# Windowed attention: key sums moved between the key blocks, scores on four 64x64 tiles, division after the values

## The chip, the core and the metric

The kernel runs on one core of a Trainium2 chip. A core has four compute engines that run side by side, each through its own queue in order: TensorE (PE: matmuls; its weight loads are listed apart as PEld), VectorE (DVE), ScalarE (ACT) and GpSimd (POOL). SyncE (SP) starts transfers. Operands lie in on-chip memory of 128 partitions; TensorE writes its results to PSUM, from where VectorE or ScalarE fetch them. The metric is the device time of one execution in microseconds, lower is better. Everything is 32-bit floating point.

## The reference

Two layers run over `x` of shape (2, 1024, 256). The change is in the attention of the second layer, and this is its reference, cut:

```python
# L = 1024, bl = 128, nb = 8 blocks, G = 64 groups of 16 tokens, H = 16 heads, dh = 64
q = einsum('bld,dhk->blhk', x, Wq) / sqrt(dh)
k = einsum('bld,dhk->blhk', x, Wk);  v = einsum('bld,dhk->blhk', x, Wv)
g = einsum('bld,lg->bgd', x, one_hot)          # sums of 16 tokens
side_k = einsum('bgd,dhk->bghk', g, Wk);  side_v = einsum('bgd,dhk->bghk', g, Wv)
# a block of queries sees its own key block, the one before, the one after, and all 64 side keys
k_cat = concatenate([k of 3 blocks, side_k]);  v_cat = ...
logits = einsum('bnqhd,bnkhd->bnhqk', qb, k_cat) + where(|distance| <= 127 and inside, 0, -1e9)
m = maximum(logits.max(-1), 0)
probs = exp(logits - m) / (exp(logits - m).sum(-1) + exp(-m))
y = einsum('bnhqk,bnkhd->bnqhd', probs, v_cat)
out = einsum('blhk,hkd->bld', y, Wo)
```

A query sees keys up to 127 places away on either side. So of the two neighbour blocks, a query at place i of its block sees the last 127 - i keys of the one before and the first i keys of the one after.

## The kernel before

The stage is `attn1` (line 1427) with `attn1_heads` (line 1538). `attn1` goes over the two batches. For each it first projects keys: for each m (a pair of heads, 8 in all) two products of 512 columns into `pq` (line 1498), copied by ScalarE to `kT` (line 1499), and the key sums `pg` from the token sums `g` (line 1504), copied to `sk`. In `kT` the 64 rows of a pair's first head are partitions 0 to 63, those of the second 64 to 127. Then it projects values (`pv`, line 1512) into `v` with keys on partitions, and the value sums into `sv` (line 1526), which holds zeros in the half that does not belong to a head. In the second batch, steps of the next adapter run beside the key projection.

`attn1_heads` then goes over 32 items: 8 query blocks n, and in each the pairs of heads m = 0, 2, 4, 6, two pairs (four heads) to an item. An item passes three steps, and the steps of three items are staggered: in one turn come `scores` of item i, `turn` of item i - 1 and `values` of item i - 2.

- `scores`: for each pair a PSUM tile `ps` of two banks, one per head. Two matmuls (line 1597), each 64 rows deep and 128 queries wide, multiply the queries with 384 keys (an inner block) or 256 (n = 0 and n = 7, called edge items here); two more (line 1601) with the 64 key sums. In an inner block, VectorE then merges one neighbour block into the place of the other where the latter is masked (predicated copies, lines 1603 and 1604), so that 320 columns are left of 448. A reduction (line 1607) adds the mask, negates and finds the maximum; ScalarE takes the exponential with its sum (line 1617), and of the maximum (`extra`). VectorE adds and inverts (`rd`, lines 1623 and 1624), and the weights `pe` are multiplied by it, the first head's on VectorE (line 1625), the second's on ScalarE (line 1626).
- `turn`: TensorE transposes the weights, ten times 128x128 an item (lines 1639 and 1640), into `pt` and `pts`. ScalarE copies the first block and the sums (lines 1643, 1649); VectorE takes the merged neighbours apart again by two products with triangles `tri` (line 1646).
- `values`: for each pair and block, the two heads' matmuls, side by side on 64 columns of the array each (line 1666), accumulate into `py`, the key sums' part last. `py` is one PSUM buffer, taken anew every second item, and ScalarE copies it to `yT` then (line 1678).

After every fourth item in turn, TensorE has a block of projections: the queries of the next two n (`queries`, lines 1564 to 1571, called before the scores of m = 4 of an odd n), or the output of the last two (`output`, lines 1688 to 1691, called behind the values of m = 6 of an odd n). Both use the two buffers of `ps`.

No order is written out by hand beyond the stagger. The framework in which the kernel is written puts in the waits and plans each engine's order: program order, with instructions that it expects to be ready earlier pulled ahead. A tile's next writer waits until its readers are done.

Of the kernel before, what the change touches and what calls it, by code (L numbers as in the profile page):

```python
# [1419 lines left out]

def load_attn1(k, pool, names):
    for n in names:
        k.w1a[n] = pool.tile([P, 2048], F32, name=f"w1a{n}")
        k.nc.sync.dma_start(out=k.w1a[n], in_=part(k.ins["w1a"], W1A, n))


def attn1(k, ci, x):
# [7 lines left out]
    with tiles(tc, name="a1r", bufs=1) as rp:  # L1435

        tri = rp.tile([P, 2, P], F32, name="tri")
        nc.gpsimd.memset(tri, 1.0)

        wbs = rp.tile([P, 4, G + 2 * P + G], F32, name="wbs")
        nc.gpsimd.memset(wbs, 0.0)
        for i in range(2):
            sign = 1 - 2 * i
            nc.gpsimd.affine_select(
                out=tri[:, i],
                in_=tri[:, i],
                compare_op=ALU.is_gt,
                fill=0.0,  # L1450
                base=0,
                pattern=[[-sign, P]],
                channel_multiplier=sign,
            )
        left, right = slice(G, G + P), slice(G + P, G + 2 * P)
        for t, op, sign in (
            (wbs[:, 0, right], ALU.is_gt, -1),
            (wbs[:, 1, right], ALU.not_equal, 1),
            (wbs[:, 2, left], ALU.not_equal, 1),
            (wbs[:, 3, left], ALU.is_gt, 1),  # L1460
        ):
            nc.gpsimd.affine_select(
                out=t, in_=t, compare_op=op, fill=-1.0e9, base=0, pattern=[[sign, P]], channel_multiplier=-sign
            )

        near = rp.tile([P, 2, P], U8, name="near")
        for i, t in enumerate((wbs[:, 3, left], wbs[:, 0, right])):
            nc.vector.tensor_scalar(near[:, i], t, 0.0, None, ALU.is_ge)
        for b in range(B):
            kT = rp.tile([P, 8, S], F32, name="kT")  # L1470
            v = rp.tile([P, NB, 1024], F32, name="v")

            g = rp.tile([P, 2, 2, G], F32, name="g")
            sk = rp.tile([P, 8, G], F32, name="sk")

            sv = rp.tile([P, 8, 2, 64], F32, name="sv")
            nc.gpsimd.memset(sv, 0.0)
            for c in range(2):
                nc.vector.reduce_sum(
                    g[:, c, 0, :], ci[:, c, b * S : (b + 1) * S].rearrange("p (g t) -> p g t", t=16), axis=AX.X  # L1480
                )
            nc.vector.tensor_copy(g[:, :, 1, :], g[:, :, 0, :])
            with ExitStack() as st:
                pp = st.enter_context(tiles(tc, name="a1a", bufs=2 if b else 3, space=PSUM))
# [6 lines left out]
                for m in range(8):  # L1491
                    ms = slice(m * P, (m + 1) * P)
                    for half in range(2):
                        ts = slice(b * S + half * CK, b * S + (half + 1) * CK)
                        ls = slice(half * CK, (half + 1) * CK)
                        pq = pp.tile([P, CK], F32, name="pq")
                        for c in range(2):
                            nc.tensor.matmul(pq, lhsT=wk[:, c, ms], rhs=ci[:, c, ts], start=c == 0, stop=c == 1)  # L1498
                        nc.scalar.copy(kT[:, m, ls], pq)
                    if beside:  # L1500
                        next(beside[m // 4])
                    pg = pp.tile([P, G], F32, name="pg", bufs=1 if b else 2)
                    for c in range(2):
                        nc.tensor.matmul(pg, lhsT=wk[:, c, ms], rhs=g[:, c, 0, :], start=c == 0, stop=c == 1)
                    nc.vector.tensor_copy(sk[:, m, :], pg)
                for half in range(2):
# [17 lines left out]
                    for i in range(2):  # L1524
                        rows = slice(i * G, (i + 1) * G)
                        nc.vector.tensor_copy(
                            sv[rows, 4 * half : 4 * half + 4, i],
                            pv[rows].rearrange("p (m i d) -> p m i d", i=2, d=64)[:, :, i],
                        )
            with (  # L1530
# [4 lines left out]
                attn1_heads(k, b, x, ci, kT, v, sk, sv, (wbs, near, tri), rp, sp, pp, yp)  # L1535
# [432 lines left out]
```

## Time and profile before

| | us |
|---|---|
| median of 3 runs | 1516.82 |
| lowest, highest | 1510.14, 1517.79 |
| the profiled execution | 1515.27 |
| its span, first to last instruction | 1513.6 |
| key projection of batch 0 begins | 876 |
| scores of batch 0, first and last item begin | 945, 1140 |
| scores of batch 1, first and last item begin | 1237, 1434 |

The two sweeps of `attn1_heads` are thus about 400 us of the span. The granted clock is 1.00 in all stretches from 875 us on. Times in the order of time count from the start of the span; the second number in such a line is a duration, "64x384" is partitions by elements, "64*128" the rows and columns of the array that a matmul uses. A 32-bit matmul leaves two records, a transpose one, and records overlap, since TensorE starts the next before the last has left: what one costs is read from start to start. In the chain that ended last, each piece is the time until the next piece could go on.

### The profile page before, as it was taken

To read this page: it belongs to the slowest core of one execution; us is meant where nothing else is said; L and a number is where in the kernel's file an instruction comes from. 1 tells how busy PE (TensorE), PEld (TensorE's weight loads), DVE (VectorE), ACT (ScalarE), POOL (GpSimd) and SP (SyncE) were. 2 spreads that over 40 slices of the span, in tenths; PEclk is the share of its full clock that TensorE was granted. 3 is DMA by queue.
4 is the path that set the end of the run, shared out by engine and by line. 5 is a ranking of instruction groups with operands and counts; after the bars stand their busy time and mean duration, and the time that the engine had idled before them with its cause. 6 is when DMAs were issued, how large, how long until landed. Compare 5 with 4: busy or idle time off the path is not lost. (4 is left out here: it accounts for less than half of the span.)

```text
span 1513.6 us, 27333 instructions
## 1 busy us (share of the span) xinstructions
PE 1414.6 (93%) x10778; PEld 964.2 (64%) x10778; DVE 872.7 (58%) x2774; ACT 680.9 (45%) x1681; POOL 180.7 (12%) x167
## 2 busy tenths in 40 slices
PE   5998889999699999968999999999999999999998
PEld 2445877445456766635666645788886457878866
DVE  3545834121489931157887713787884247778764
ACT  2443143222122122117888721766674337656733
POOL 1523630022411121110000000000000000000011
PEclk9899589999899999979999999999999999999999
DMA  9500004300353332030000010000000000000001
GB/s 307 188 1 2 5 2 154 125 30 30 95 166 120 127 129 82 18 121 1 2 2 2 29 56 1 2 2 2 1 2 1 0 0 2 2 1 2 2 15 44
DMA packets 42758, 70.77 MB, mean 47 GB/s; under 512 B 7168, under 2 KB 35840, under 8 KB 39552
## 3 DMA queue, kind: packets, MB, share of 16 engines
q1 hardware_dynamic: 35776, 55.55, 11.0%
q0 software_dynamic: 3072, 8.65, 1.6%
q10 hardware_dynamic: 3776, 4.75, 1.0%
q8 instruction: 87, 1.43, 0.4%
q14 instruction: 47, 0.39, 0.1%
HBM read 45.09 MB, written 23.86 MB: 46 GB/s over the span
## 5 line engine op out<-in xcount | busy, mean ns | idle before, releaser
L1617 ACT ACTIVATE pe<-pe,nm 128x320 f32<-128x320 f32 x256 | 141.8, 555 | 131.1 <-DVE nm L1607 130.9
L1607 DVE CUSTOM_DVE_ANT_0 pe<-ps,wbs 128x320 f32<-128x320 f32 x256 | 118.5, 486 | 6.1 <-PE ps L1601 1.8
L1229 ACT ACTIVATE pe<-pe,nm 128x256 f32<-128x256 f32 x256 | 110.4, 498 | 20.4 <-DVE nm L1219 20.4
L965 PE MATMUL ph<-xt,w 128*128 128x512 f32 x256 | 113.8, 602 | 2.7 <-ACT xt L960 2.7
L1597 PE MATMUL ps<-kT,qT 64*128 64x384 f32 (+1 forms) x512 | 110.2, 498 | 3.3 <-DVE qT L1571 2.9
L973 PE MATMUL po<-w,h 128*128 128x256 f32 x512 | 111.8, 379 | 0.0
L973 PEld LDWEIGHTS po<-w,h 128*128 128x128 f32 x512 | 97.3, 190 | 16.6 <-issue 3.3
L1219 DVE CUSTOM_DVE_ANT_0 pe<-ps,lc 128x256 f32<-128x256 f32 x256 | 94.2, 417 | 21.0 <-PE ps L1203 19.3
L1666 PE MATMUL py<-ptt,v 128*64 128x128 f32 x1408 | 103.6, 277 | 0.1
L895 DVE SCALAR_TENSOR_TENSOR lc<-iok,idx,lc 128x256 f32<-128x256 f32 x248 | 102.2, 475 | 0.3
L965 PEld LDWEIGHTS ph<-xt,w 128*128 128x128 f32 x256 | 48.6, 193 | 62.6 <-issue 55.7
L1666 PEld LDWEIGHTS py<-ptt,v 128*64 128x64 f32 x1408 | 78.6, 137 | 11.3 <-issue 8.3
L1639 PE MATMUL pt<-ident,pe 128*128 128x128 f32 x512 | 79.8, 282 | 1.9 <-DVE pe L1625 0.9
L1238 PE MATMUL ptp<-ident,pe 128*128 128x128 f32 x512 | 73.8, 283 | 5.7 <-ACT pe L1229 2.9
L1238 PEld LDWEIGHTS ptp<-ident,pe 128*128 128x128 f32 x512 | 55.8, 142 | 33.1 <-ACT pe L1229 16.8
L968 ACT ACTIVATE h<-ph,vecs 128x512 f32<-128x512 f32 x64 | 44.0, 687 | 71.3 <-PE ph L965 70.2
L1626 ACT ACTIVATE pe<-pe,rd 128x320 f32<-128x320 f32 x128 | 70.8, 558 | 8.9 <-DVE rd L1624 8.9
L1601 PEld LDWEIGHTS ps<-sk,qT 64*128 64x128 f32 x512 | 50.9, 187 | 26.2 <-issue 0.3
L1646 DVE TENSOR_TENSOR ptt<-pt,tri 128x512 f32<-128x512 f32 x96 | 64.8, 675 | 0.0
L1639 PEld LDWEIGHTS pt<-ident,pe 128*128 128x128 f32 x512 | 56.1, 140 | 10.9 <-issue 2.0
L976 DVE TENSOR_TENSOR ye<-po,b 128x256 f32<-128x256 f32 x32 | 13.4, 419 | 82.4 <-PE po L973 82.4
L1688 PE MATMUL ps<-yT,w1ao 128*128 128x256 f32 x256 | 59.0, 385 | 0.7
(355 smaller groups left out, 2743.5 us busy)
## 6 DMA issues: line engine op xcount, KB each, us to landing
w<-in_mw SPq DMA_DIRECT2D x16, 1024.0 KB, 5.2
xs<-z SPq DMA_DIRECT2D x8, 1088.0 KB, 11.8
ys<-z SPq DMA_DIRECT2D x4, 1024.0 KB, 11.6
xe<-xs SPq DMA_DIRECT2D x7, 544.0 KB, 6.3
more<-xs SPq DMA_DIRECT2D x7, 544.0 KB, 4.0
x<-in_xT ACTq DMA_DIRECT2D x4, 512.0 KB, 5.9
g<-ys ACTq DMA_DIRECT2D x4, 512.0 KB, 6.0
out_x<-o SPq DMA_DIRECT2D x8, 256.0 KB, 2.2
```

Of the source, the lines that this page charges most:

```text
L895: nc.vector.scalar_tensor_tensor(n, key, k.idx[:, qb, j : j + 1], n, ALU.is_equal, ALU.add)
L965: nc.tensor.matmul(ph, lhsT=w1[:, c, m * P : (m + 1) * P], rhs=xt[:, c, :], start=c == 0, stop=c == 1)
L973: nc.tensor.matmul(po, lhsT=h[:, m, j * P : (j + 1) * P], rhs=w2[:, m, :], start=m == 0, stop=m == 7)
L1219: nc.vector.tensor_tensor_reduce(out=pe[:, j, :], in0=it["ps"][i][:, j, :], in1=k.lc[:, q0 + j, :], scale=-1.0, scalar=3.0e38, op0=ALU.add ...
L1229: nc.scalar.activation(pe[:, j, :], pe[:, j, :], AF.Exp, bias=nm, scale=-1.0)
L1238: nc.tensor.transpose(ptp[:, kb, j, :], it["pe"][i][:, j, kb * P : (kb + 1) * P], k.ident)
L1597: nc.tensor.matmul(ps[:, i, keys[i]], lhsT=qs[i], rhs=kT[hp, m + pair, k0 : k0 + nk], start=True, stop=True)
L1607: nc.vector.tensor_tensor_reduce(out=pe[:, i], in0=ps[:, i, used[i]], in1=wbs[:, 0 if n == 0 else 3 if n == NB - 1 else 1 + i, (1 - i) * G ...
L1617: nc.scalar.activation(pe[:, i], pe[:, i], AF.Exp, bias=nm[:, i : i + 1], scale=-1.0, accum_out=den[:, i : i + 1])
L1626: nc.scalar.activation(pe[:, 1], pe[:, 1], AF.Copy, scale=rd[:, 1:2])
L1639: nc.tensor.transpose(pt[1 - j if i and inner(n) else j][:, 2 * pair + i, :], pe[:, at : at + P], k.ident)
L1666: nc.tensor.matmul(py[64 * i : 64 * i + 64, (m + pair) % 4, :], lhsT=keys[:, hs], rhs=it["pts"][:, pair, :] if j == 3 else it["pt"][:, j, ...
```

## The change

1. `kT` grows by 256 columns, and each head gets its own order of columns, with copies of the 64 key sums between key blocks, so that for every query block a run of 448 columns (320 at the edges) holds its key blocks and one copy of the sums. A class `Keys` holds the two orders; `view` finds, for a head and a block, where the run starts, which 320 columns are used, and which block is merged into which.
2. The key sums come no longer from a matmul with `g`, but from a reduction of `pq` over 16 tokens on VectorE; ScalarE copies the first head's rows of `pq`, VectorE the second's, and GpSimd copies the sums into `kT` after m = 3 and m = 7. `g` and `sk` live only while projecting.
3. Scores: four matmuls a pair, one for each head and half of the queries, each on a 64x64 quarter of the array. A half of the queries leaves out the 64 keys at the far end that are masked for all of it, so that most have 384 columns with the sums in them (320 at the edges).
4. The merge becomes two predicated copies per head, one of all 128 queries by 64 keys, one of 64 by 64.
5. The weights are not divided. Addition and reciprocal are done once an item for four heads; ScalarE spreads the reciprocals over 64 columns a head (`rdw`); two more transposes in `turn` turn them into the second half of `pts`.
6. The key sums' values become a step `sums` of their own, before `turn`: four matmuls on 64x64 quarters, which open the accumulation; `sv` loses its zeros. `py` is one tile for the whole batch. After its last block, each item's two slots of `py` are multiplied by the turned reciprocals into `yT`, by VectorE.
7. The query scaling moves from VectorE to ScalarE; `tri` goes, and the triangle masks `near` (one byte each) take its place.

```diff
+class Keys:
+    def __init__(self, order):
+        self.at, self.sums, at = {}, [], 0
+        for n in order:
+            if n is None:
+                self.sums.append(at)
+                at += S // 16
+            else:
+                self.at[n] = at
+                at += P
...
+KEYS = [Keys([0, 1, None, 2, 3, None, 4, 5, None, 6, 7]), Keys([None, 0, 1, 2, None, 3, 4, None, 5, 6, 7, None])]
...
+def window(n):
+    first = 0 if n == 0 or n in (1, 3, 5) else 1
+    return [KEYS[i].view(i, n, first ^ i) for i in range(2)]
...
-            kT = rp.tile([P, 8, S], F32, name="kT")
+            kT = rp.tile([P, 8, S + 4 * G], F32, name="kT")
...
-                        pq = pp.tile([P, CK], F32, name="pq")
+                        pq = pp.tile([P, CK], F32, name="pq", bufs=3)
...
-                        nc.scalar.copy(kT[:, m, ls], pq)
+                        nc.vector.reduce_sum(sk[:, m, gs], pq.rearrange("p (g t) -> p g t", t=16), axis=AX.X)
+                        for i in range(2):
+                            hp = slice(64 * i, 64 * i + 64)
+                            for n0, n1 in KEYS[i].runs(4 * half, 4 * half + 4):
...
+                                copy = nc.vector.tensor_copy if i else nc.scalar.copy
+                                copy(kT[hp, m, at : at + w], pq[hp, o : o + w])
...
-                    pg = pp.tile([P, G], F32, name="pg", bufs=1 if b else 2)
-                    for c in range(2):
-                        nc.tensor.matmul(pg, lhsT=wk[:, c, ms], rhs=g[:, c, 0, :], start=c == 0, stop=c == 1)
-                    nc.vector.tensor_copy(sk[:, m, :], pg)
+                    if m % 4 == 3:
+                        for i in range(2):
+                            hp = slice(64 * i, 64 * i + 64)
+                            for at in KEYS[i].sums:
+                                nc.gpsimd.tensor_copy(kT[hp, m - 3 : m + 1, at : at + G], sk[hp, m - 3 : m + 1])
...
-            nc.vector.tensor_scalar_mul(qT[:, m : m + 4, :], pq, 0.125)
+            nc.scalar.activation(qT, pq, AF.Copy, scale=0.125)
...
+            for half in range(2):
+                qs = slice((n % 2) * P + half * 64, (n % 2) * P + half * 64 + 64)
+                for hp, view in zip(hps, views):
+                    c0, c1 = view.parts[half]
+                    nc.tensor.matmul(
+                        ps[hps[half], view.head, c0:c1],
+                        lhsT=rows["qT", n // 2, m // 4][hp, (m + pair) % 4, qs],
+                        rhs=kT[hp, m + pair, view.start + c0 : view.start + c1],
...
+                    both, one = (slice(0, 64), slice(64, P)) if view.kind == 0 else (slice(64, P), slice(0, 64))
+                    for rs, cs in ((slice(0, P), both), (one, one)):
+                        nc.vector.copy_predicated(
+                            ps[rs, i, to + cs.start : to + cs.stop],
+                            near[rs, view.kind, cs],
+                            ps[rs, i, of + cs.start : of + cs.stop],
+                        )
...
-            nc.vector.tensor_scalar_mul(pe[:, 0], pe[:, 0], rd[:, 0:1])
-            nc.scalar.activation(pe[:, 1], pe[:, 1], AF.Copy, scale=rd[:, 1:2])
+        nc.vector.tensor_add(rd, den, extra)
+        nc.vector.reciprocal(rd, rd)
+        it["rd"] = sp.tile([P, 4, 64], F32, name="rdw")
+        nc.scalar.copy(it["rd"], rd.unsqueeze(2).to_broadcast([P, 4, 64]))
...
+        for pair in range(2):
+            rd = it["rd"][:, 2 * pair : 2 * pair + 2].rearrange("p i d -> p (i d)")
+            nc.tensor.transpose(pts[:, 1, pair, :], rd, k.ident)
...
-                nc.vector.tensor_mul(ptt[:, 1 + i], pt[1], tri[:, i : i + 1, :].to_broadcast([P, 4, P]))
+                nc.vector.tensor_mul(ptt[:, 1 + i], pt[1], near[:, i : i + 1, :].to_broadcast([P, 4, P]))
...
+    py = yp.tile([P, 4, P], F32, name="py")
+    def sums(it):
...
+                nc.tensor.matmul(
+                    py[64 * view.head : 64 * view.head + 64, (m + pair) % 4, :],
+                    lhsT=sv[hs, views[0].place, m + pair, :],
+                    rhs=it["pts"][hs, 0, pair, :],
+                    start=pair == 0,
...
-            nc.scalar.copy(rows["yT"][:, m - 3 : m + 1, ns], py)
+        nc.vector.tensor_mul(rows["yT"][:, m : m + 2, ns], py[:, m % 4 : m % 4 + 2], it["pts"][:, 1])
...
-    staggered(items, scores, turn, values)
+    for i in range(len(items) + 2):
+        for j, step in ((0, scores), (2, sums), (1, turn), (2, values)):
+            if 0 <= i - j < len(items):
+                step(items[i - j])
```

## The prediction

> **What bounds the kernel now.** I read the busy shares first, then the granted clock, then the stage by its stretches, then the order of time on each engine, then the chain that ended last.
>
> ```profile
> PE 1414.6 (93%) x10778; PEld 964.2 (64%) x10778; DVE 872.7 (58%) x2774; ACT 680.9 (45%) x1681; POOL 180.7 (12%) x167
> ```
>
> TensorE is busy 93% of the span, VectorE 58%. That average says little about this stage. From 945 us on, the table by stretches (us, PE, PEld, DVE, ACT, POOL busy, clock) has this line for a stretch of items without a query or output block:
>
> ```profile
> 1010.00:1026.00 16.00, 16.00 (x197) 13.23 (x192) 15.38 (x61) 13.09 (x44) 0.00 (x0) 1.00 0.01 2
> ```
>
> TensorE is busy for 16.00 of 16.00 us, but VectorE for 15.38 as well, at full clock. The order of time shows both, for one inner item (two pairs of heads), TensorE first:
>
> ```profile
> 1016.17 0.92 PE L1597 MATMUL ps<-kT,qT 64*128 64x384 f32 x4
> 1016.92 0.33 PE L1601 MATMUL ps<-sk,qT 64*128 64x64 f32 x4
> 1017.09 0.87 PE L1597 MATMUL ps<-kT,qT 64*128 64x384 f32 x4
> 1017.79 0.34 PE L1601 MATMUL ps<-sk,qT 64*128 64x64 f32 x4
> 1018.05 0.66 PE L1639 MATMUL pt<-ident,pe 128*128 128x128 f32 x4
> ...
> 1019.29 0.88 PE L1666 MATMUL py<-ptt,v 128*64 128x128 f32 x12
> 1020.00 0.39 PE L1666 MATMUL py<-ptts,sv 128*64 128x128 f32 x4
> 1020.22 0.83 PE L1666 MATMUL py<-ptt,v 128*64 128x128 f32 x12
> ...
> 1021.19 0.92 PE L1597 MATMUL ps<-kT,qT 64*128 64x384 f32 x4
> ```
>
> From start to start: scores 1.88 us (16.17 to 18.05), transposes 1.24, values 1.90, together 5.02 per item. VectorE in the same time:
>
> ```profile
> 1012.59 0.29 DVE L1603 COPY_PREDICATED ps<-near,ps 128x128 f32<-128x128 uint8 x1
> 1012.91 0.30 DVE L1604 COPY_PREDICATED ps<-near,ps 128x128 f32<-128x128 uint8 x1
> 1013.24 0.49 DVE L1607 CUSTOM_DVE_ANT_0 pe<-ps,wbs 128x320 f32<-128x320 f32 x1
> ...
> 1017.91 0.29 DVE L1603 COPY_PREDICATED ps<-near,ps 128x128 f32<-128x128 uint8 x1
> ```
>
> Its item takes 5.32 us, 0.3 more than TensorE's. It falls behind by 0.3 per item, and catches up only in the blocks of 7.2 us of projection that TensorE runs after every fourth item, the queries (L1564) and the outputs (L1688) in turn. The chain that ended last shows that this is already just enough in one burst of two: between a query block and an output block it runs on VectorE, then over ScalarE's copy of the result into the output:
>
> ```profile
> 1034.56 0.30 DVE ps L1603
> ...
> 1051.29 0.49 DVE pe L1607
> ...
> 1055.49 0.49 ACT yT L1678
> ...
> 1056.03 5.45 PE ps L1688 x24
> ```
>
> So TensorE bounds the bursts that end in queries, and VectorE those that end in an output.
>
> **TensorE, part by part.** (1) Scores. The two records of 384 columns of a pair take 0.75 and 0.70 us, the key sums 0.17 to 0.26 behind them. Now four 64x64 tiles of 384 columns do both. That four such tiles run at once is seen in the first attention: there 39 records of 64x32 (L432, such tiles in the same order) took 1.29 us, although one lasts 0.29. I take 0.70 and 0.65 for the pairs. (2) The key sums' values leave the second block (L1666 on ptts, 0.22 per pair) and become four 64x64 matmuls of the same 128 columns behind the scores: 0.44, plus 0.1 for the change to transposes. Scores with sums are then 1.89 against 1.88, and values lose 0.44. (3) Two transposes more, at 0.11 each (four took 0.44 from 1018.65 to 1019.09): +0.22. An inner item goes from 5.02 to about 4.80. In the 16 edge items the scores keep 320 columns where they had 256 and 64, and the same terms cancel: 0. (4) The projection of key sums (L1504) goes: eight key records fill 3.44 us and the next m begins 3.88 after the last, so 0.44 x 16 = 7.0 us.
>
> **VectorE, per inner item.** Each merge becomes two of 64 columns, 8 instead of 4. They don't overlap what follows (0.33 from start to start for a duration of 0.29). A 64-column merge isn't in the trace: its price lies between the reciprocal on 2 columns (0.16) and the 128-column merge (0.29); I take 0.225, by the 64-column copy from PSUM (L1505, 0.220), so 0.26 from start to start: 8 x 0.26 - 4 x 0.33 = +0.76. The weights' scaling goes (0.30 from start to start, twice): -0.60. One addition and reciprocal for four heads, not two: -0.15. The product into yT (128x256 from PSUM, like L552, 0.418, less the overlap of some 0.05) is new: +0.37. Together 5.32 + 0.38 = 5.70; with the ends for the merge 5.2 to 6.2. The query scaling (1.22, L1571) leaves VectorE, but it ran inside the query block, where VectorE idles: nothing gained.
>
> **ScalarE and GpSimd.** ScalarE loses two scalings (0.56 each) and the yT copy (0.58 per two items), and gains the reciprocal broadcast (256 columns, 0.36), 256 more columns in the ptts copy (0.21), and the query scaling, which holds the second score buffer after a block as VectorE's did (0.52 before): lighter, no bound. GpSimd gets 14 small copies of key sums per batch, two groups of seven; at the 0.3 to 1.1 us of its rows they end under the 30 us of value projection. It loses a memset and tri. No DMA changes.
>
> **Key projection.** Per m TensorE has 3.44 us. VectorE gets two reductions of 512 columns (0.69 each, by L1518) and four 64-partition copies (0.56 and 0.29): 3.1 us, where it was busy 1.34 of 20. In batch 1 the adapter adds about 1 us per m on either engine. Three buffers cover it: 0, and 2 us of loss if not.
>
> **Where the stalls go.** An inner item of 4.80 against 5.70 makes VectorE fall behind by 0.9 per item rather than 0.3. Three things are in its favour: the weights reach the transposes without the scaling behind them, the query scaling is gone, and the reciprocals are needed last. Against it stands a new wait: py is now one tile for the whole batch, and yT is made from it for every item by VectorE. The next item's key sums write py, so they wait for that product; behind them on TensorE stand the transposes and the values. Before, ScalarE read py every second item, and TensorE waited for it 0.6 us in all. From the last value matmul to the next sums lie only the next scores, 1.35 us, less 0.3 until VectorE sees the result and 0.4 of product.
>
> I take that wait to hold for the whole of py, although the next item writes other slots of it.
>
> The Trainium skill has a rule here (PSUM — Partial Sum Buffer, "PSUM bank collisions raise a hardware error"): engines are to be kept apart by bank, not by address. The four slots of py fill one 2 KiB bank, so by the page even another slot's product holds the sums back; were it by slot, the bursts ending in queries below would gain 0.9 each instead of losing 0.6, and the sum would be 6 us lower.
>
> Burst from queries to output (six times): first merge 0.98 after the first scores, then four VectorE items of 5.70 to the product that the output needs, or three and the fourth's four merged reductions (4 x 0.93) and the product, if that is ordered first: 0.98 + 21.2 to 22.8 = 22.2 to 23.8. Now the output starts 20.6 after those scores (1033.31 to 1053.9). That is +1.6 to +3.2; I take the middle, 2.4, because the planner does change the order where VectorE is late (at 1251 us it put transposes between the matmuls of two score pairs): +14.4. Bursts from output to queries (four times): nothing needs the last product, but the sums of items two to four need the one before. VectorE ends the products at 6.7, 12.4 and 18.1 after the first scores; TensorE wants them at 6.15, and then, each 4.80 after the last wait, at 11.6 and 17.3: waits (with 0.1 of signalling) of 0.65, 0.9 and 0.9, so 4 x 4.80 + 2.45 = 21.6 where it is 20.0 now: +1.6. If the transposes, which don't need py, are put ahead of the sums, most of it goes: +0.2. I take 0.6: +2.4. Other inner items (8): -1.8. Shorter start of the two batches: -1. Key sums' projection: -7.0. **Sum: +7.0 us**, on the profiled execution's 1515.27 us (span 1513.6 and 1.7 around it), which is 1.55 under the median of the runs, 1516.82: **1522 us**, with a range of its own from 1513 to 1532.
>
> **Rivals.** *TensorE stays the bound* (0.26): merges at the low end, or an order in which VectorE's lag is always hidden: 48 x 0.22 + 7.0 + 1.5 = 19 less, 1496 us. For it: over eight items VectorE needs 46 us of TensorE's 53. It decides once a VectorE item is under about 5.3. This is the side of a gain. *VectorE sets every inner item* (0.20): the product stands behind the next item's merges, so that bursts ending in queries pay too: 48 x (5.70 - 5.02) = 33, less 9: 1539. The stretch with DVE 15.38 of 16.00 speaks for it, the idle 7 us blocks against. *The tiles don't run four at once* (0.04): a pair pays its 0.65 twice, 48 x 2 x 0.65 + 16 x 2 x 0.5 = 78 more: about 1600; L432 speaks against it.
>
> A rule weighed: TensorEngine Tiling (Array Packing), "PSUM Bottleneck", says that tiling speeds up TensorE but not the emptying of PSUM. The trace agrees in this stage (5.32 against 5.02). Taken as the whole truth it gives the second rival's 1539; the trace's blocks give 1522.
>
> **How the numbers follow.** My case 0.50, the rivals 0.26, 0.20, 0.04. Half a per cent, about what a measurement of this kernel can tell from no change, is 7.6 us. Of my case, 0.03 lies below 1509, 0.28 within, 0.19 above 1524. Faster 0.29, same 0.28, slower 0.43. The range takes in the first two rivals: 1494 to 1539.
>
> **What would show it.** Right: pairs of scores 0.7 us apart with eight records; VectorE items of 5.6 to 5.8; TensorE idle before the sums or the output, released by VectorE's yT; no L1504. Wrong: a 64-column merge under 0.19 us, TensorE without gaps at 4.8 (first rival), or score pairs of 1.3 us (third).

## The result: 0.6% slower, near the forecast, with another wait behind it

| | us |
|---|---|
| before, median (lowest, highest) | 1515.61 (1510.14, 1524.36) |
| after, median (lowest, highest) | 1524.97 (1523.03, 1527.70) |
| ratio, with its 95% interval | 1.0056 (1.0038 to 1.0074) |
| profiled execution of after, and its span | 1523.03, 1521.3 |

The forecast was 1522, so the sum came out 3 us off. Two of its steps were wrong, and they are the ones worth reading about: TensorE does wait for VectorE, but at another place than forecast, and VectorE's item is long for another reason.

To see where the time went, the stage is cut at the first records of its steps: start of a key projection, first scores, first scores of an inner block (n = 1), of the last edge block (n = 7), and of the last item. In us:

| | before | after | difference |
|---|---|---|---|
| projection before the first scores, batch 0 | 68.94 | 66.35 | -2.59 |
| first four items (n = 0) | 16.59 | 15.11 | -1.48 |
| the 24 inner items | 164.95 | 172.28 | +7.33 |
| first to last item of n = 7 | 13.40 | 14.21 | +0.81 |
| last item to the next projection | 17.31 | 17.73 | +0.42 |
| projection, batch 1 | 79.14 | 77.55 | -1.59 |
| first four items | 15.25 | 16.22 | +0.97 |
| the 24 inner items | 169.07 | 172.18 | +3.11 |
| first to last item of n = 7 | 13.40 | 14.21 | +0.81 |
| last item to the last output | 15.79 | 16.20 | +0.41 |

Together +8.2: the two sweeps over the items +11.6, the projections -4.2, the ends +0.8. The spans differ by 7.7; the rest lies outside these stages: the stage begins 2.4 us earlier in the trace of after, and what follows the last output takes 2.0 longer, with the same code in both.

### The profile page after: what moved, and what is told of

It is laid out like the page before. It is cut to its first block, busy times and chain, and to the rows that moved or that the text cites. A ratio compares the mean times of both kernels' runs of the same rounds, so it can differ in the third digit from the quotient of the medians.

```text
span 1521.3 us, 27492 instructions
## 1 busy us (share of the span) xinstructions
PE 1404.2 (92%) x10842; PEld 919.8 (60%) x10842; DVE 893.6 (59%) x2846; ACT 664.6 (44%) x1569; POOL 189.0 (12%) x189
## 5 line engine op out<-in xcount | busy, mean ns | idle before, releaser
L1641 PE MATMUL ps<-kT,qT 64*64 64x384 f32 (+2 forms) x1024 | 109.7, 494 | 21.2 <-DVE nm L1662 18.2
L1654 DVE COPY_PREDICATED ps<-near,ps 64x64 f32<-64x64 uint8 (+1 forms) x384 | 79.5, 226 | 39.4 <-PE ps L1641 32.0
L1735 PE MATMUL py<-ptt,v 128*64 128x128 f32 x1408 | 91.0, 277 | 0.0
L1735 PEld LDWEIGHTS py<-ptt,v 128*64 128x64 f32 x1408 | 75.5, 137 | 10.7 <-issue 10.7
L1641 PEld LDWEIGHTS ps<-kT,qT 64*64 64x64 f32 x1024 | 29.8, 131 | 71.3 <-PE ps L1641 38.0
L1705 DVE TENSOR_TENSOR ptt<-pt,near 128x512 f32<-128x512 f32 x96 | 65.4, 681 | 0.5 <-PE pt L1695 0.5
L202 POOL TENSOR_TENSOR both<-x 128x512 f32<-128x512 f32 x8 | 10.6, 1326 | 405.3 <-issue 401.1
```

Of the source, the lines that this page charges most:

```text
L1641: nc.tensor.matmul(ps[hps[half], view.head, c0:c1], lhsT=rows["qT", n // 2, m // 4][hp, (m + pair) % 4, qs], rhs=kT[hp, m + pair, view.sta ...
L1654: nc.vector.copy_predicated(ps[rs, i, to + cs.start : to + cs.stop], near[rs, view.kind, cs], ps[rs, i, of + cs.start : of + cs.stop],)
L1735: nc.tensor.matmul(py[64 * i : 64 * i + 64, (m + pair) % 4, :], lhsT=keys[j][:, hs], rhs=it["pt"][:, j, 2 * pair + i, :], start=False, sto ...
```

## The profile after

The busy shares of the page have hardly moved:

```profile
PE 1404.2 (92%) x10842; PEld 919.8 (60%) x10842; DVE 893.6 (59%) x2846; ACT 664.6 (44%) x1569; POOL 189.0 (12%) x189
```

The table by stretches has moved, for the same 16 us of inner items without a projection block that were read before the change (us, busy time of PE, PEld, DVE, ACT, POOL, granted clock, DMA share, GB/s):

```profile
1010.00:1026.00 16.00, 14.20 (x158) 10.67 (x157) 13.98 (x56) 10.82 (x34) 0.00 (x0) 1.00 0.00 1
```

TensorE was busy for all of the 16.00 us, and is now idle for 1.80. VectorE is not full either: 13.98, where it was 15.38. Neither engine is full, so one waits for the other and that one for a third. The order of time shows TensorE's side, at the end of a line what it waited for:

```profile
1011.52 0.88 PE L1641 MATMUL ps<-kT,qT 64*64 64x384 f32 x8
1013.26 0.88 PE L1641 MATMUL ps<-kT,qT 64*64 64x384 f32 x8 [0.86 <-DVE nm L1662]
1013.97 0.60 PE L1718 MATMUL py<-ptts,sv 64*64 64x128 f32 x8
1014.50 0.66 PE L1695 MATMUL pt<-ident,pe 128*128 128x128 f32 x4
...
1015.96 1.53 PE L1735 MATMUL py<-ptt,v 128*64 128x128 f32 x24
1017.42 0.88 PE L1641 MATMUL ps<-kT,qT 64*64 64x384 f32 x8
1019.23 0.88 PE L1641 MATMUL ps<-kT,qT 64*64 64x384 f32 x8 [0.94 <-DVE nm L1662]
```

Eight records start within one pair's 0.70 us: the four tiles do run at once. Without the wait an item is 0.70 + 0.70 + 0.53 (key sums) + 1.46 (transposes) + 1.46 (values) = 4.85. But the second pair of scores waits 0.86 to 0.94 until VectorE's reduction (`nm`) has emptied the score buffer of the item before. In each block of four items this happens in the third and the fourth. Over the run, the group of the scores has this line (busy us, mean ns, idle time before and what ended it):

```profile
L1641 PE MATMUL ps<-kT,qT 64*64 64x384 f32 (+2 forms) x1024 | 109.7, 494 | 21.2 <-DVE nm L1662 18.2 <-ACT qT L1621 2.5
```

Before, the scores' idle time was 3.3 us in all. VectorE's side of the same item:

```profile
1012.62 0.49 DVE L1662 CUSTOM_DVE_ANT_0 pe<-ps,wbs 128x320 f32<-128x320 f32 x1
1013.03 0.08 DVE L1662 DVE_READ_ACCUMULATOR2_ANT nm<- 128x1 f32 x1
1013.03 0.42 DVE L1746 TENSOR_TENSOR yT<-py,ptts 128x256 f32<-128x256 f32 x1
1013.93 0.16 DVE L1679 TENSOR_TENSOR rd<-den,extra 128x4 f32<-128x4 f32 x1 [0.48 <-ACT extra L1677]
1014.13 0.23 DVE L1654 COPY_PREDICATED ps<-near,ps 128x64 f32<-128x64 uint8 x1
1014.27 0.17 DVE L1680 RECIPROCAL rd<-rd 128x4 f32<-128x4 f32 x1
1014.47 0.24 DVE L1654 COPY_PREDICATED ps<-near,ps 64x64 f32<-64x64 uint8 x1
...
1015.27 0.75 DVE L1654 COPY_PREDICATED ps<-near,ps 128x64 f32<-128x64 uint8 x4
1016.06 0.49 DVE L1662 CUSTOM_DVE_ANT_0 pe<-ps,wbs 128x320 f32<-128x320 f32 x1
...
1019.00 0.42 DVE L1746 TENSOR_TENSOR yT<-py,ptts 128x256 f32<-128x256 f32 x1
```

From product to product 5.97 here and 5.85 in the next item, 5.91 on average of the two (5.57 to 6.14 over the inner items within blocks of four). 0.48 of it is idle: the addition of the item's four sums stands right behind the last reduction and the product, and waits until ScalarE has taken the exponential of what that reduction left, and of the four maxima. Behind it stand the merges of the next scores, which have been ready for long. So the circle is: last reduction, ScalarE, addition, merges, reductions, score buffer, TensorE.

The output, which the forecast had waiting for the last product, starts behind the values without a gap. TensorE's lines, then VectorE's:

```profile
1050.85 1.53 PE L1735 MATMUL py<-ptt,v 128*64 128x128 f32 x24
1052.31 7.17 PE L1756 MATMUL ps<-yT,w1ao 128*128 128x256 f32 x32
```

```profile
1053.82 0.42 DVE L1746 TENSOR_TENSOR yT<-py,ptts 128x256 f32<-128x256 f32 x1
```

The last product comes 1.5 us after the output has begun. The output runs over m = 0 to 7, and needs this product's two slots only for m = 6 and 7.

## The experiments

In the traces of the experiments the stage begins between 873.4 and 880.3 us, although the layers before it are the same code; medians can differ by this too. So each verdict goes by the lengths of the stages above, "inner" for the 24 inner items (172.28 and 172.18 after), and the ratio to before, taken on the same chip, is given with it.

### The key sums by reduction, alone

```diff
 # in the kernel before
+gs = slice(half * G // 2, (half + 1) * G // 2)
+nc.vector.reduce_sum(sk[:, m, gs], pq.rearrange("p (g t) -> p g t", t=16), axis=AX.X)
...
-pg = pp.tile([P, G], F32, name="pg", bufs=1 if b else 2)
-for c in range(2):
-    nc.tensor.matmul(pg, lhsT=wk[:, c, ms], rhs=g[:, c, 0, :], start=c == 0, stop=c == 1)
-nc.vector.tensor_copy(sk[:, m, :], pg)
```

> The kernel before with one part of the change alone: the key sums are reduced on VectorE from the projected keys (two reductions of 0.69 us per m), the matmuls of the key sums and their copy go, the projection's buffers become three. Theory (the prediction's term): TensorE loses 16 times 0.44 us and the reductions hide under the 3.44 us of projection per m, so 7.0 us less than before, between 5 and 9. Rival: the projection is paced by emptying its buffers, and the time stays within 2 us of before or rises.

Measured: 1511.05 us, ratio 0.9976 (0.9954 to 0.9998). The projections take 65.37 and 76.79 us, 3.57 and 2.35 less than before, 5.9 in all; the sweeps stay at 194.95 and 197.73. The theory holds. In batch 0 the step is 8 x 0.44 as forecast; in batch 1, where the adapter's steps run between, a third less. The changed kernel gains only 4.2 of these 5.9 us; the run with four buffers, below, explains 1.0 of the 1.7 that are missing.

### Two more transposes an item

```diff
+for _ in range(2):
     nc.tensor.transpose(pts[:, 1, pair, :], rd, k.ident)
```

> The changed kernel with each item's two transposes of the reciprocals done twice: 64 items get two transposes of 0.11 us more, on TensorE alone. Theory: VectorE's item of 5.85 us sets the pace of the inner items and TensorE, at 4.86, waits for score buffers, so the change is small: 0 to 5 us more than the changed kernel. Rival: TensorE's own work sets the pace, and it takes all of 64 x 0.22 = 14 us more.

Measured: 1535.82 us, ratio 1.0127 (1.0100 to 1.0155). The inner items take 175.75 and 175.62 us, 3.5 and 3.4 more, 0.145 an item, and the whole stage 8.8 more: over the theory's 5, under the rival's 14. VectorE's order of time tells what it is:

```profile
1018.66 0.16 DVE L1679 TENSOR_TENSOR rd<-den,extra 128x4 f32<-128x4 f32 x1 [0.48 <-ACT extra L1677]
1018.86 0.18 DVE L1680 RECIPROCAL rd<-rd 128x4 f32<-128x4 f32 x1
1019.07 0.51 DVE L1654 COPY_PREDICATED ps<-near,ps 128x64 f32<-128x64 uint8 x2
1019.61 0.49 DVE L1662 CUSTOM_DVE_ANT_0 pe<-ps,wbs 128x320 f32<-128x320 f32 x1
```

The planner has put the reciprocal directly behind the addition, where it stood between the two merges of one head. From addition to reduction it is 0.95 us in this item, instead of 0.81. That 0.14 is of the size of the 0.145 per item, although TensorE's own item grew by 0.22 as well; TensorE still waits 0.86 in the third and the fourth item of this block. So the run does not show TensorE as the bound; but it was not the clean test that it was meant to be, as the order of another engine changed with it.

### One merge of 128 columns, all 448 columns of scores

```diff
-            v.parts = [
-                (0, size - P // 2 * (self.at[near[-1]] + P == start + size)),
-                (P // 2 * (self.at[near[0]] == start), size),
-            ]
...
-for rs, cs in ((slice(0, P), both), (one, one)):
-    nc.vector.copy_predicated(ps[rs, i, to + cs.start : to + cs.stop], near[rs, view.kind, cs], ...)
+nc.vector.copy_predicated(ps[:, i, to : to + P], near[:, view.kind], ps[:, i, of : of + P])
```

> The changed kernel with one merge of 128 columns per head, where it has two of 64, and so all 448 columns of scores computed for both halves of the queries. VectorE loses 8 x 0.27 and gains 4 x 0.33 us per inner item, -0.84; TensorE's pairs of scores grow by a sixth of 0.70, +0.23 per item, to 5.1. Theory (VectorE sets the pace): 10 to 22 us less than the changed kernel. Rival (TensorE sets it): 48 x 0.23 = 11 us more.

Measured: 1507.18 us, ratio 0.9940 (0.9917 to 0.9962), so 18 us under the changed kernel and 9 under the one before; the stage alone is 18.2 us shorter than in the changed kernel. The inner items take 163.81 us in both batches, 8.5 and 8.4 less. TensorE now does more work per item and has no gap, as its order of time and the table by stretches show:

```profile
1004.37 1.74 PE L1637 MATMUL ps<-kT,qT 64*64 64x448 f32 x16
1005.93 0.60 PE L1710 MATMUL py<-ptts,sv 64*64 64x128 f32 x8
...
1009.38 1.74 PE L1637 MATMUL ps<-kT,qT 64*64 64x448 f32 x16
```

```profile
1005.00:1021.00 16.00, 16.00 (x183) 11.85 (x176) 14.69 (x53) 12.34 (x38) 0.00 (x0) 1.00 0.00 1
```

A 448-column pair takes 0.78, so an item 5.01 (1004.37 to 1009.38), and that is its pace. The theory holds: in the changed kernel VectorE sets the pace of the inner items, and without the halves of the merges its lag no longer reaches TensorE. From 945 to 1145 us TensorE waits 1.6 us in all, where it was 10.6 in the changed kernel, and 0 of it for the product into `yT`.

### Addition and reciprocal on GpSimd

```diff
-nc.vector.tensor_add(rd, den, extra)
-nc.vector.reciprocal(rd, rd)
+nc.gpsimd.tensor_add(rd, den, extra)
+nc.gpsimd.tensor_tensor(out=rd, in0=rd, in1=k.one4, op=ALU.pow)   # one4 holds -1
```

> The changed kernel with the addition and the reciprocal of the sums on GpSimd (as a power of -1). VectorE loses 0.33 us of work per item and the 0.48 us in which it waits for ScalarE's exponential of the maxima in front of the addition. Theory: that wait stands in VectorE's chain, which sets the inner items, so an item of VectorE falls from 5.85 to 5.04 us, and the time falls by 15 to 26 us, to 1499 to 1510, under the kernel before. Rival 1: TensorE's waits come from the one buffer of the results, not from VectorE's load: within 4 us of the changed kernel. Rival 2: only the busy 0.33 us counts, since the wait would be spent later in any case: 6 to 10 us less.

Measured: 1533.95 us, ratio 1.0109 (1.0079 to 1.0138): slower, and none of the three. Of the 7.8 us between the profiled executions 5.0 are the stage's later start; the stage itself takes 3.0 more. The inner items do get shorter, 167.87 and 167.73, 4.4 less per batch. VectorE has no gap in front of its merges any more, and its item is 5.36 and not 5.04: without the wait alone it would be 5.43 (5.91 less 0.48), so that taking the addition and the reciprocal, 0.33 us of work, off VectorE gained only 0.07 beyond the wait. What it gains is paid back at the ends, where no lag of VectorE hides a longer chain: the first four items 18.70 and 18.42 (15.11 and 16.22 after), those of n = 7 15.50, the two ends behind the last item 1.75 more each. The wait has moved to ScalarE, whose queue holds the exponentials of the next item behind it. First GpSimd, then ScalarE:

```profile
1015.91 0.20 POOL L1681 TENSOR_TENSOR rd<-den,extra 128x4 f32<-128x4 f32 x1 [10.87 <-ACT extra L1679]
1016.19 1.01 POOL L1682 TENSOR_TENSOR rd<-rd,one 128x4 f32<-128x4 f32 x1
```

```profile
1015.64 0.19 ACT L1679 ACTIVATE extra<-nm 128x4 f32<-128x4 f32 x1
1017.23 0.40 ACT L1684 COPY rdw<-rd 128x256 f32<-128x256 f32 x1 [1.40 <-POOL rd L1682]
```

### The product left out

```diff
-nc.vector.tensor_mul(rows["yT"][:, m : m + 2, ns], py[:, m % 4 : m % 4 + 2], it["pts"][:, 1])
+nc.scalar.copy(rows["yT"][:, m : m + 2, ns], py[:, m % 4 : m % 4 + 2])
```

> The changed kernel without the multiplication by the turned reciprocals: ScalarE copies the two slots of the result into the output's operand, so the weights stay undivided (this part of the computation is left out). VectorE loses 0.42 us of work per item, in the same order otherwise. Theory: the product stands between the last reduction and the addition, which waits for ScalarE's exponentials of that same reduction, 0.90 us; so the product lies in a gap, VectorE's idle time in front of the addition goes from 0.48 to 0.90, and the time falls by 0 to 4 us only. Rival 1 (each busy microsecond of VectorE counts): 48 x 0.42 = 20 us less. Rival 2 (the prediction's wait for the one result buffer sets the pace, and a copy by ScalarE holds it as long or longer): no less, or more.

Measured: 1531.27 us, ratio 1.0087 (1.0065 to 1.0109). The inner items take 172.17 and 172.19 us, against 172.28 and 172.18. VectorE has 0.42 us less to do in each of them, and nothing changes:

```profile
1017.83 0.08 DVE L1662 DVE_READ_ACCUMULATOR2_ANT nm<- 128x1 f32 x1
1018.73 0.16 DVE L1679 TENSOR_TENSOR rd<-den,extra 128x4 f32<-128x4 f32 x1 [0.82 <-ACT extra L1677]
```

From the last reduction's result to the addition it is 0.90 us, with the product and without it. The theory holds, rival 1 falls. The profiled execution is above the changed kernel's mainly because the stage starts 4.8 us later in this trace (878.58) and what follows it is 1.6 us longer; no part of the stage is longer by more than 0.7, and the whole of it by 1.2.

### Two constants added instead of the sums

```diff
-nc.vector.tensor_add(rd, den, extra)
+nc.vector.tensor_add(rd, k.one4, k.one4)
```

> The changed kernel in which the addition in front of the reciprocal adds two constants and not the sums of the exponentials (so the division is left out of the computation; all instructions stay, on the same engines). VectorE then need not wait for ScalarE in front of it. VectorE's order changes in one place: the reciprocal stands directly behind the addition, as in the run with two more transposes, which cost 0.14 us per item there. Theory (the 0.48 us of waiting stand in VectorE's chain, which sets the inner items): an inner item falls from 5.91 to 5.43 + 0.14 = 5.57 to 5.63 us, the six inner blocks of a batch from 172.3 to 164 to 166 us, in all 12 to 17 us less than the changed kernel. Rival (the wait is spent elsewhere once it is gone, for the score buffers or the result): inner blocks within 1.5 us of 172.3.

Measured: 1519.19 us, ratio 1.0005 (0.9985 to 1.0024). The inner items take 168.56 and 168.71 us, 3.7 and 3.5 less; both sweeps together fall by 9.4. VectorE's item is 5.54, under what the theory said, but only half of the gain arrives:

```profile
1010.96 0.42 DVE L1748 TENSOR_TENSOR yT<-py,ptts 128x256 f32<-128x256 f32 x1
1011.29 0.15 DVE L1681 TENSOR_TENSOR rd<-one 128x4 f32<-128x4 f32 x1
1011.48 0.18 DVE L1682 RECIPROCAL rd<-rd 128x4 f32<-128x4 f32 x1
...
1016.49 0.42 DVE L1748 TENSOR_TENSOR yT<-py,ptts 128x256 f32<-128x256 f32 x1
```

```profile
1016.72 0.88 PE L1643 MATMUL ps<-kT,qT 64*64 64x384 f32 x8 [0.50 <-DVE nm L1664]
...
1022.26 0.88 PE L1643 MATMUL ps<-kT,qT 64*64 64x384 f32 x8 [0.50 <-DVE nm L1664]
```

TensorE's two waits per block of four go from 0.86 and 0.94 to 0.50 and 0.50. My expectation multiplied the 0.3 us by all items. But a block starts with free score buffers, and its first two items run ahead of VectorE whatever that takes; and behind the fourth come 7 us of projection, in which VectorE catches up (it idles 5.38 us there in the changed kernel, 6.41 in this one). So a block loses only the lag that exceeds the buffers, 0.8 us less in this block and 0.6 on the average of the six. That the wait stands on the path is shown; its price is 9 us of the sweeps.

### The division where it was

```diff
+extra = sp.tile([P, 2], F32, name="extra", bufs=3)
+nc.scalar.activation(extra, nm[:, two], AF.Exp)
+nc.vector.tensor_add(rd, den[:, two], extra)
+nc.vector.reciprocal(rd, rd)
+    nc.scalar.activation(pe[:, j], pe[:, j], AF.Copy, scale=rd[:, 1:2])     # second head
+    nc.vector.tensor_scalar_mul(pe[:, j], pe[:, j], rd[:, 0:1])             # first head
...
-    nc.tensor.transpose(pts[:, 1, pair, :], rd, k.ident)
...
-nc.vector.tensor_mul(rows["yT"][:, m : m + 2, ns], py[:, m % 4 : m % 4 + 2], it["pts"][:, 1])
+nc.scalar.copy(rows["yT"][:, m : m + 2, ns], py[:, m % 4 : m % 4 + 2])
```

> The changed kernel with the division put back where it was: addition and reciprocal per pair, the weights scaled by VectorE (first head) and ScalarE (second), the results copied by ScalarE; scores, merges, key sums and projection stay as changed. VectorE per inner item: +0.60 for two scalings, +0.37 for two more small operations, -0.42 product; TensorE -0.22 (two transposes less). Theory (VectorE sets the pace): an item of 6.0 to 6.2 us for 5.9, 5 to 15 us more than the changed kernel. Rival (TensorE sets it): 64 x 0.22 = 14 us less.

Measured: 1537.58 us, ratio 1.0122 (1.0101 to 1.0143). The inner items take 175.79 and 179.36 us, the two sweeps 8.5 us more than in the changed kernel. The rival falls: TensorE has 14 us less to do, and the time rises. The size is the theory's, but its cause is not shown by this run. TensorE's waits in the first sweep (945 to 1155 us; us in total, times, longest) begin with these two:

```profile
PE py L1720 <- ACT yT L1748: 4.6, 12, 0.7
PE ps L1641 <- DVE nm L1662: 2.4, 4, 0.7
```

The key sums wait most, for ScalarE's copy of `py` into `yT`. That copy reads the two slots of the item before, while the sums write the other two, and they start 0.05 us after its end. So this is the wait that the prediction expected for the product, with another engine in VectorE's place. How much of the 8.5 us is VectorE's greater load and how much is this wait, the run doesn't separate. Of the change's parts, then, the undivided weights help, against this form of the division, and the merges in halves hurt.

### The triangles on GpSimd

```diff
-for i in range(2):
-    nc.vector.tensor_mul(ptt[:, 1 + i], pt[1], near[:, i : i + 1, :].to_broadcast([P, 4, P]))
+nc.vector.tensor_copy(both, pt[1])
+for i in range(2):
+    nc.gpsimd.tensor_mul(ptt[:, 1 + i], both, k.tri[:, i : i + 1, :].to_broadcast([P, 4, P]))
```

> The changed kernel with the two products with triangles moved to GpSimd: VectorE only copies the merged block out of PSUM (0.6 us) where it made two products (1.3 us), -0.7 per inner item, 5.9 to 5.2, against 4.86 on TensorE. GpSimd needs about 2 x 1.1 us, by its products of 128x512 elsewhere. Theory (VectorE sets the pace): 10 to 25 us less than the changed kernel, 1500 to 1515. Rival: GpSimd's 2.2 us come too late for the values, or slow VectorE down, and the time stays within 4 us or rises.

Measured: 1532.77 us, ratio 1.0103 (1.0079 to 1.0126); the inner items take 172.95 and 172.92 us, 0.7 more than in the changed kernel. The rival holds, and in its second half: GpSimd holds VectorE up. VectorE's addition of four columns, and GpSimd's two products:

```profile
1019.64 0.80 DVE L1681 TENSOR_TENSOR rd<-den,extra 128x4 f32<-128x4 f32 x1 [0.48 <-ACT extra L1679]
...
1025.78 0.80 DVE L1681 TENSOR_TENSOR rd<-den,extra 128x4 f32<-128x4 f32 x1 [0.48 <-ACT extra L1679]
```

```profile
1017.92 2.50 POOL L1709 TENSOR_TENSOR ptt<-both,tri 128x512 f32<-128x512 f32 x2 [3.78 <-DVE both L1707]
1024.06 2.50 POOL L1709 TENSOR_TENSOR ptt<-both,tri 128x512 f32<-128x512 f32 x2 [3.64 <-DVE both L1707]
```

The addition takes 0.16 elsewhere and 0.80 here, and it ends when GpSimd ends: 1020.44 and 1020.42, 1026.58 and 1026.56. With this 0.64 VectorE's item is 6.1 to 6.3 us. That is more than 5.2 and 0.64; the merges, between which the products stood, now stand back to back, and I take the rest to be that, but no run separates it. (The run also has one buffer for `rdw`, where the changed kernel has two.)

### One merge, and four buffers for the projected keys

```diff
-pq = pp.tile([P, CK], F32, name="pq", bufs=3)
+pq = pp.tile([P, CK], F32, name="pq", bufs=3 if b else 4)
```

> The kernel with one merge per head, with four buffers for the projected keys in the first batch where it has three. Theory: in that projection TensorE waits 4.0 us for ScalarE's copies, which wait for VectorE's reduction of the same buffer (0.69 us), and that makes the projection 1.0 us longer than in the kernel before with the reductions alone, 66.36 against 65.37; with four buffers it falls to 65.4 to 65.8, the rest stays, the time is 1 us under the run with one merge, 1504 to 1509. Rival: the copies are too slow altogether (not only late), so a fourth buffer only moves the wait, and the projection stays at 66.3.

Measured: 1504.75 us, ratio 0.9914 (0.9885 to 0.9943). The projection of batch 0 takes 65.37 us, as with the reductions alone; all else in the stage is unchanged to 0.01. The theory holds. In the changed kernel each buffer is read by VectorE's reduction first, and ScalarE's copies wait for that; with three buffers TensorE's weight loads then wait for ScalarE (in the view of waits, for the 67 us of that projection: us in total, times, longest):

```profile
ACT kT L1547 <- DVE sk L1540: 20.3, 16, 1.8
...
PEld pq L1538 <- ACT kT L1547: 4.0, 6, 0.8
```

### One merge, and 384 columns

```diff
+two = [pp.tile([P, 2, CK], F32, name=f"ps{i}", bufs=1) for i in range(2)]   # taken in turn by bank()
...
-ps = pp.tile([P, 2, CK], F32, name="ps")
+ps = bank()
...
+nc.vector.copy_predicated(ps[:, i, to : to + P], near[:, view.kind], ps[:, i, of : of + P])
```

> One merge of 128 columns per head, four key buffers as before, but the scores keep the 384 columns of the changed kernel: the two score buffers are the same two tiles for the whole batch, so that the columns left out hold older scores, which the merge's mask passes over. TensorE's item is then 4.86 us again where it is 5.02 with one merge and 448 columns; VectorE's stays at about 5.07 (5.91 less 0.84). Theory: with one merge TensorE alone sets the pace (it waits 1.6 us in all in the first sweep), so its work counts now: between nothing of the 0.16 per item, if VectorE's 5.07 takes over at once, and all of it, 24 x 0.16 = 3.8 us per batch; the first two items of each block of four run ahead of VectorE and the blocks of projection let it catch up, so most of it: inner blocks from 163.81 to 160 to 161.5, the time 5 to 8 us less than the run with one merge and four buffers. Rival: VectorE is at its limit there too, and the inner blocks stay within 0.5 us of 163.8.

Measured: 1500.71 us, ratio 0.9880 (0.9853 to 0.9907): the fastest of the runs, 18 us under the kernel before. The inner items take 160.49 and 160.48 us, as the theory said; of its 5 to 8 us in the median 4 are seen, with the stage starting at 878.96. TensorE's order of time, then VectorE's:

```profile
1017.63 1.52 PE L1646 MATMUL ps<-kT,qT 64*64 64x384 f32 x16
1018.98 0.60 PE L1719 MATMUL py<-ptts,sv 64*64 64x128 f32 x8
...
1020.97 1.53 PE L1736 MATMUL py<-ptt,v 128*64 128x128 f32 x24
1022.43 7.17 PE L1619 MATMUL ps<-c,w1aq 128*128 128x256 f32 x32
```

```profile
1018.31 0.41 DVE L1747 TENSOR_TENSOR yT<-py,ptts 128x256 f32<-128x256 f32 x1
1018.78 0.16 DVE L1680 TENSOR_TENSOR rd<-den,extra 128x4 f32<-128x4 f32 x1
1018.98 0.18 DVE L1681 RECIPROCAL rd<-rd 128x4 f32<-128x4 f32 x1
...
1023.34 0.41 DVE L1747 TENSOR_TENSOR yT<-py,ptts 128x256 f32<-128x256 f32 x1
```

TensorE's item is 4.80 us (1017.63 to 1022.43), VectorE's 5.03. VectorE still falls behind by 0.23 an item, but a block of four ends before the buffers run out, and no wait of TensorE for it is left in the inner items. The addition hardly waits any more either (0.06 us, between 1018.72 and 1018.78): with fewer merges the planner's order has a product with a triangle between the last reduction and the product into `yT`.

## Why the prediction was right, and where it was not

**TensorE's item: right.** "From 5.02 to about 4.80": 4.85 where nothing waits in the changed kernel, 4.80 with one merge and 384 columns. Four tiles do run at once (0.70 and 0.68 a pair), so the third rival is out.

**VectorE's item: 5.70 forecast, 5.91 measured, and the terms are not those.** The length of a merge was right (0.226 us by the group's mean, 0.225 taken), and the run with one merge shows that the merges decide. But they overlap more than was taken: four in a row need 0.79 us (1015.27 to 1016.06), 0.20 each, where 0.26 stood in the sum. The term that failed is "One addition and reciprocal for four heads, not two: -0.15". I counted instructions, and not what the one addition waits for. For four heads it needs the exponential of the item's last reduction, 0.90 us after that reduction; so it adds a gap. The other failed term is the product's +0.37: it stands in that gap and costs nothing, as the run without it shows. Without the gap the item would be 5.43, less than forecast.

**Where TensorE waits: wrong.** The step was that the next item's key sums wait for the product, since `py` is one tile. In no item of the trace do they: they start 0.39 us or more after the product has ended, and the view of waits has no line of that kind. They come behind the scores, and these wait first, for the score buffers. I had worked with VectorE's lag, but not asked which buffer that lag fills; it was `ps`, with two buffers for two pairs an item. The wait as such exists: in the run with the division the sums wait 4.6 us in a sweep for a copy of the item before, which reads the other slots of `py`. That agrees with the rule of the Trainium skill that I weighed there (PSUM — Partial Sum Buffer, "PSUM bank collisions raise a hardware error"), that engines are to be kept apart by bank and not by address. In the changed kernel it just never comes last.

**Blocks of four: the sum right, the split wrong.** Queries to output were to lose 2.4, output to queries 0.6. Measured from first scores to first scores: items 14 to 18 take 28.93 where they took 28.09, +0.84; items 10 to 14 take 29.09 where they took 27.19, +1.90. The first was wrong at "to the product that the output needs": the output needs it only for its last two m. The second is too small for the wait on the score buffers, which both kinds of block have. Two blocks together: 2.74, forecast 3.0.

**Both sweeps: +14.0 forecast, +11.6 measured.** In batch 0 the inner items lose 7.33, in batch 1 only 3.11, although they take the same 172.2 us in both. It is the kernel before that differs: its batch 1 has the item that I had seen at 1251 us, with transposes between the matmuls of a pair. From that item's scores to the next it is 8.71 us where batch 0 has 4.59, and this 4.1 us is gone now. I had seen it and given it no price.

**Projection: -7.0 forecast, -4.2 measured.** Removing the matmuls brings 5.9, 1.1 less than 16 x 0.44, because batch 1 hides part of them; and the copies cost 1.7, by the runs with and without a fourth buffer 1.0 of it in batch 0; what the 0.8 of batch 1 are, no run shows. The prediction had named this ("Three buffers cover it: 0, and 2 us of loss if not") and taken the wrong one of its two values.

So +11.6 - 4.2 + 0.8 = +8.2 stands against the forecast +7.0: two terms were each some 2.5 us too large, with opposite signs, and the ends had no term. That the time came out so near is thus in part luck: without the 4.1 us of batch 1 the sweeps alone would have lost 15.7 against the 14.0. The first rival, TensorE as the bound, was put at a VectorE item "under about 5.3": the runs have waits for VectorE's reductions at 5.54, 1.0 us of them in a sweep at 5.36, and none in the inner items at 5.03, and with 5.03 the time is 1500.7 us, where that rival said 1496. The second, VectorE in every item, fails because the blocks of projection do let it catch up: it idles 5.4 us in one. The rule under "PSUM Bottleneck" (TensorEngine Tiling (Array Packing)), that tiling doesn't speed up the emptying of PSUM, agrees with the changed kernel (an item of 4.85 on TensorE, of 5.91 on VectorE); as the whole truth, 1539, it was too much.

## What to carry to other kernels

When instructions of several groups are merged into one, the merged one needs the last of its inputs; price the wait in front of it by the chain that makes that input, and what already lies in this gap is free. When an engine falls behind, ask which buffer its lag fills, and count only the lag that the buffers and the next pause don't take up. Saving work on the full engine by giving work to the one just behind it can lose more than it saves, and a cheaper form (here one merge over columns that needn't be computed) can keep both gains.

## What the hardware showed

- An addition of 128x4 on VectorE, both operands in on-chip memory, took 0.80 us instead of 0.16 while GpSimd multiplied 128x512 blocks there, and ended within 0.02 us of GpSimd. VectorE's products and reductions from PSUM ran beside GpSimd at their usual length (0.42 and 0.49). The Trainium skill has this (SBUF — State Buffer, "SBUF: two separate sides"): VectorE and GpSimd share a pair of ports, held by one of them for a whole instruction; a VectorE operation with two inputs in that memory needs it. The trace agrees.
- A 64-column merge takes 0.23 us. The next VectorE instruction starts 0.13 to 0.14 us after the merge's start in some places, and only behind its end, 0.24 to 0.27 after its start, in others. Needing its result is one reason, but not the only one: no merge needs a product with a triangle, and yet in block n = 1 of the changed kernel, where all 64-row merges lie on partitions 64 to 127, every merge behind such a product starts 0.72 us after the product's start, behind its end, and in n = 6, where they lie on partitions 0 to 63, every one starts after 0.60, before its end. So the partitions at which neighbours begin go with it; no run changes them alone. A reciprocal between the two merges of a head lengthened the way from the one to the other by 0.1 us or less, and by its place behind the addition the way to the reduction by 0.14 in the item shown.
- GpSimd took 1.01 us for a power of 128x4, and 0.20 for an addition of that size.
- The start of the stage differs by up to 7 us between the profiled executions, with the same code ahead of it (873.4 to 880.3 us). The mean granted clock over the span goes with it: 0.962 to 0.964 in the three that begin before 874, 0.955 to 0.960 in the five that begin after 878.5, and 0.959 to 0.963 in the four between. Which comes first, the runs don't show. In the stage itself the clock is 1.00.
